# Tokens in chunks of eight rows ahead of layer 1's scans, and layer 0's depthwise conv as diagonal products on TensorE

## The chip, the cores and the metric

The kernel runs on one core of one Trainium2 chip. The time is device microseconds from the first to the last instruction of an execution, the median of several executions. The kernel before took 1817.63 us (1816.01 to 1822.36) when the prediction was made. "Clock" is the share of full speed that was granted to TensorE.

## The reference, cut to what matters

Two layers over 64 x 64 tokens of 96 features. Each layer is a state-space mixer with a residual addition and an MLP with quantized operands with another. Both have the gate, the output norm belongs to layer 0 alone; layer 0's conv is depthwise, layer 1's is a full 192 x 192 one.

```
# layer 0's mixer (the input is normed per token first)
xz = x @ in_proj_w                        # 96 -> 192 and a gate z of 192
xc = conv3x3_depthwise(x_val) + conv_b    # layer 1: dense 3x3, 192 -> 192
u  = silu(xc)
y  = y1 + y2 + back(y3) + back(y4)        # four scans: rows, columns, both ways
y  = layernorm(y, ln_g, ln_b) * silu(z)   # layer 1: no norm here
x  = x + y @ out_proj_w
# the MLP, on a normed x: 96 -> 384 -> 96, fp8 operands
h = relu(q_acc(q_mul(x) @ q_mul(W1).T + q_mul(b1)))
x = x + q_acc(q_mul(h) @ q_mul(W2).T + q_mul(b2))
```

In layer 0 the scan's form, `decay * cumsum(dB_u / (decay + 1e-12))`, makes the output vanish once the decay has run down. The kernel computes the first 160 tokens of each direction, tests whether any later one can matter (`alive`), and for this data skips the rest behind a branch. ln_b is zero and ln_g one in this data.

## The kernel before: the parts concerned

Each phase runs over all 4096 tokens before the next one starts. A norm is five or six instructions over 128 x 3072 elements, and the MLP follows as a loop of eight chunks:

```python
    def norm_tokens(self, pool, eps, dtype):
        # ...
        nc.vector.tensor_reduce(m, res, AX.X, ALU.add)            # 128 x 3072 at once
        # ... centre, square, reduce, root, reciprocal
        nc.vector.tensor_tensor(xn, xc, spread(r), ALU.mult, saturate=False)

    def mlp(self, li, w, out):
        # ...
            xq = self.norm_tokens(wp, self.eps5, FP8)             # all tokens
            # ...
            for b in range(NJ // 4):                              # eight chunks
                # four transposes, a copy, three hidden products with copy, relu, cast,
                # twelve output products, copy, bias, residual
```

Layer 0's conv is VectorE's, nine multiply-adds per channel group:

```python
    def conv_depthwise(self, kp, w, pad, u):
        # ...
                    nc.vector.scalar_tensor_tensor(acc, src, cw[:, tap : tap + 1], acc, ALU.mult, ALU.add)
```

The output product takes 128 tokens as TensorE's weights and moves the 96 columns of the matrix past them:

```python
                for q in range(4):
                    for g in range(2):
                        nc.tensor.matmul(t[:, q, :], by_j[g][:, 4 * b + q, :], self.w_out[g], start=g == 0, stop=g == 1)
```

## Time and profile before

| stage of the kernel before | from | to | us |
|---|---|---|---|
| layer 0 up to the branch (norm, projection, conv, first tokens' scans) | 0 | 218 | 218 |
| layer 0 from the branch to layer 1's conv | 218 | 466 | 248 |
| layer 1's conv and projections | 466 | 668 | 202 |
| transfers alone | 668 | 711 | 43 |
| layer 1's scans | 711 | 1663 | 952 |
| tail (gate, output product, MLP of layer 1) | 1663 | 1815 | 152 |

The bounds are read from a table of windows, of which the prediction shows the lines. Two more lines of that table are the MLP's norm over all tokens, and the eight MLP chunks after it with the store, at the end of the kernel (columns: stretch, length, busy us and count of PE, PEld, DVE, ACT, POOL, clock, DMA share, GB/s).

```profile
1763.00:1784.00 21.00, 0.00 (x0) 0.00 (x0) 14.88 (x13) 4.37 (x3) 2.74 (x1) 0.50 0.07 16
1784.00:1815.00 31.00, 20.23 (x152) 11.54 (x152) 19.97 (x40) 20.05 (x40) 16.73 (x24) 0.67 0.15 52
```

### The profile page before, as it was taken

What the parts mean: (1) busy time and instruction counts of PE and PEld (TensorE: products, weight loads), DVE (VectorE), ACT (ScalarE), POOL (GpSimd) and SP (SyncE); (2) the same over time, 40 slices, a digit from 0 to 9 for tenths busy, and PEclk for the clock granted to TensorE, in tenths of its full rate; (3) what the DMA queues carried; (4) which work ended last, traced back from release to release, by engine and by line L of the source; (5) the groups of instructions that cost most, each with busy time, mean ns of one, the idle gap of its engine ahead of it and who ended that gap; (6) DMA issues with size and microseconds to landing.
All of it is one profiled execution on the core that took longest, in us unless ns stands there. A gap on an engine that the chain in (4) does not pass through costs nothing.

```text
span 1815.0 us, 10479 instructions
## 1 busy us (share of the span) xinstructions
PE 1161.1 (64%) x3146; PEld 468.8 (26%) x3146; DVE 1297.5 (71%) x789; ACT 857.4 (47%) x900; POOL 756.3 (42%) x397
## 2 busy tenths in 40 slices
PE   3102679933999910567677657777667777666784
PEld 2000322622434300222232222222222222222262
DVE  3997367264105053999999999999999999992626
ACT  3023022043104143677766677766677766661205
POOL 0001021031001014676677776677776677752004
PEclk9555565565999955778888888888888888878556
DMA  2014100002002258145434644533553353313301
GB/s 78 0 46 132 36 0 0 0 8 78 5 1 70 75 146 324 46 142 195 139 105 154 205 139 151 185 116 105 178 204 116 139 197 116 104 47 81 116 8 36
DMA packets 52359, 182.39 MB, mean 100 GB/s; under 512 B 24080, under 2 KB 27812, under 8 KB 43940
## 3 DMA queue, kind: packets, MB, share of 16 engines
q1 hardware_dynamic: 44524, 178.44, 29.4%
q10 hardware_dynamic: 7768, 3.19, 0.8%
q8 instruction: 27, 0.44, 0.1%
q14 instruction: 40, 0.33, 0.1%
HBM read 156.39 MB, written 25.19 MB: 100 GB/s over the span
## 4 chain that ended last, share of the span: by engine, by line
DVE 41%; PE 17%; DMA 5%; ACT 4%; issue 4%; SPq 2%; POOL 2%; DVEq 1%; ACTq 1%; POOLq 0%
DVE h0s L798 12%; DVE h1s L798 11%; DVE xws L798 6%; DVE x0s L798 4%; PE cv L337 4%; DVE x1s L798 3%; PE o L1060 2%; DVE x2s L798 2%; PE cv L342 2%; PE cw L349 2%; ACT da L786 2%; SPq L742 2%; DMA dt1s<-dt 1%; PE hs L815 1%; DMA ysa<-y 1%
## 5 line engine op out<-in xcount | busy, mean ns | idle before, releaser
L815 PE MATMUL hs<-hss,ident 128*128 128x512 f32 x384 | 232.4, 690 | 131.9 <-POOL hss L804 89.8
L786 ACT ACTIVATE da<-dt0s,a 128x1024 f32<-128x1024 f32 x168 | 187.6, 1117 | 137.5 <-DVE xws L798 52.3
L786 ACT ACTIVATE da<-dt1s,a 128x1024 f32<-128x1024 f32 x168 | 187.8, 1118 | 114.8 <-DVE xws L798 77.6
L804 POOL TENSOR_TENSOR hss<-h1s,xws 128x1024 f32<-128x1024 f32 x96 | 224.4, 2375 | 23.7 <-DVE xws L798 12.6
L798 DVE TENSOR_TENSOR_SCAN xws<-da,xws 128x1024 f32<-128x1024 f32 x96 | 224.2, 2335 | 8.3
L816 PE MATMUL hs<-h0s,ident 128*128 128x512 f32 x384 | 221.4, 661 | 5.1 <-DVE h0s L798 5.1
L798 DVE TENSOR_TENSOR_SCAN h1s<-da,h1s,xws 128x1024 f32<-128x1024 f32 x72 | 169.2, 2350 | 9.5
L815 PEld LDWEIGHTS hs<-hss,ident 128*128 128x128 f32 x384 | 74.4, 211 | 272.7 <-issue 104.2
L418 POOL TENSOR_TENSOR du<-u,dts 128x1024 f32<-128x1024 f32 x6 | 17.3, 2883 | 231.5 <-DVE dts L530 227.2
L816 PEld LDWEIGHTS hs<-h0s,ident 128*128 128x128 f32 x384 | 81.5, 213 | 114.3 <-issue 102.5
L828 POOL TENSOR_TENSOR hc0s<-hc0s,cs 128x1024 f32<-128x1024 f32 x32 | 75.4, 2357 | 81.3 <-ACT hc0s L823 67.8
L828 POOL TENSOR_TENSOR hc2s<-hc2s,cs 128x1024 f32<-128x1024 f32 x32 | 75.4, 2357 | 78.2 <-ACT hc2s L823 67.9
L828 POOL TENSOR_TENSOR hc1s<-hc1s,cs 128x1024 f32<-128x1024 f32 x32 | 75.4, 2355 | 77.8 <-ACT hc1s L823 64.9
L1113 POOL CAST xb<-lnxn 128x3072 bf16<-128x3072 fp8e5 x2 | 5.5, 2742 | 207.4 <-DVE lnxn L143 119.9
L798 DVE TENSOR_TENSOR_SCAN h1s<-da,xws 128x1024 f32<-128x1024 f32 x24 | 54.7, 2278 | 51.6 <-DMA cs<-bc 48.1
L769 POOL TENSOR_TENSOR x0s<-x0s,dus 128x1024 f32<-128x1024 f32 x32 | 75.0, 2357 | 37.7 <-DMA dus<-du 26.3
L839 PE MATMUL acc<-hc0s,fold 128*32 128x512 f32 x128 | 40.6, 719 | 76.2 <-POOL hc0s L828 76.2
L839 PE MATMUL acc<-hc1s,fold 128*32 128x512 f32 x128 | 40.6, 719 | 75.2 <-POOL hc1s L828 75.2
L839 PE MATMUL acc<-hc2s,fold 128*32 128x512 f32 x128 | 39.7, 704 | 67.5 <-POOL hc2s L828 67.5
L769 POOL TENSOR_TENSOR x2s<-x2s,dus 128x1024 f32<-128x1024 f32 x32 | 75.1, 2358 | 13.5 <-DMA cs<-bc 8.0
L769 POOL TENSOR_TENSOR x1s<-x1s,dus 128x1024 f32<-128x1024 f32 x32 | 75.1, 2362 | 12.5 <-DMA cs<-bc 8.2
L775 ACT COPY xws<-x0s 128x1024 f32<-128x1024 f32 x32 | 61.5, 1952 | 36.2 <-DMA x1s<-bc 36.2
(193 smaller groups left out, 2414.9 us busy)
## 6 DMA issues: line engine op xcount, KB each, us to landing
cs<-bc SPq DMA_DIRECT2D x384, 128.0 KB, 2.6
x0s<-bc SPq DMA_DIRECT2D x32, 512.0 KB, 4.9
x1s<-bc SPq DMA_DIRECT2D x32, 512.0 KB, 4.9
x2s<-bc SPq DMA_DIRECT2D x32, 512.0 KB, 4.9
dus<-du SPq DMA_DIRECT2D x24, 512.0 KB, 7.9
dt1s<-dt SPq DMA_DIRECT2D x40, 256.0 KB, 3.9
dt0s<-dt SPq DMA_DIRECT2D x40, 256.0 KB, 3.1
u<-u SPq DMA_DIRECT2D x3, 2048.0 KB, 6.3
```

The lines of the kernel that those rows point to most:

```text
L337: nc.tensor.matmul(t, cw[0][:, tap, 0:P], image(0, slice(0, P), n, tap), start=tap == 0, stop=False)
L342: nc.tensor.matmul(t, cw[1][r, tap, 0:P], image(1, r, n, tap), start=False, stop=tap == 8)
L349: nc.tensor.matmul(out[m][to], cw[0][:, tap, P:DI], image(0, slice(0, P), c + m + h * half, tap), start=tap == 0, stop=False,)
L769: keep(nc.gpsimd.tensor_tensor(x, x, du[:, part[j]], ALU.mult))
L775: keep(nc.scalar.copy(grid(xw)[:, w, :], cols(xs[i % 3])[:, w, :]))
L786: nc.scalar.activation(das[i, s], dt[o][:, part[j]], AF.Exp, scale=self.a6[:, g, k : k + 1])
L798: keep(nc.vector.tensor_tensor_scan(to, da, x, start, ALU.mult, ALU.add))
L804: nc.gpsimd.tensor_tensor(cols(hs)[:, w, :], grid(first[1])[:, w, :], grid(xw)[:, w, :], ALU.add)
L815: keep(nc.tensor.matmul(t, self.ident, hs[:, s], start=True, stop=False))
L816: keep(nc.tensor.matmul(t, self.ident, first[0][:, s], start=False, stop=False))
L828: keep(nc.gpsimd.tensor_tensor(t, t, c[:, part[j]], ALU.mult))
L839: nc.tensor.matmul(accs[g][GC * q : GC * q + GC, m // NQ, :], self.fold4, hcs[(NS * i + a) % 3][:, h * CH : (h + 1) * CH], start=k == 0, s ...
```

## The change

The intent: tokens flow in chunks of 512 (eight rows), so that the norm, the products and the MLP of different chunks overlap on different engines, and no phase waits for all tokens. Layer 0's conv leaves VectorE: it becomes nine products with diagonal matrices on TensorE, 64 x 64 so that four run at a time, and the image's edges go first, so that the first tokens' scans start early and run beside the rest. The gate and a product of gate and norm bias move ahead of the branch. The scattered column writes of layer 1's step sizes become whole rows. The core of the diff, with cuts and with comments added:

```diff
+    def norm_chunk(self, pool, c, eps, dtype, name):   # 128 x 384, one chunk
     ...
+            ue = self.conv_ends(ep, pm, pad)            # the edges' conv
+            x = self.scan_ends(ep, pe, ue)              # first tokens, on VectorE
+            self.conv0(vp, pm, pad)                     # the whole conv, on TensorE
+            self.gate0(vp, pm, xt, pad)                 # gate, and its product with the bias
+            self.add_ends(pm, x)                        # 80 short products sum the states
     ...
-                    nc.vector.scalar_tensor_tensor(
-                        acc, src, cw[:, tap : tap + 1], acc, ALU.mult, ALU.add
-                    )
+                        nc.tensor.matmul(ab[c][r], self.diag[0][r, tap], self.image(pad, 0, r, c, tap), **ends)
     ...
+            def after(s):
+                c0 = s // 2 * 4 + s % 2
+                for c in (c0, c0 + 2):
+                    self.mlp_chunk(0, c, tp, lp, po, ph, pt)
+                    xn = self.norm_chunk(lp, c, self.eps6, F32, f"c{c}")
     ...
+                    self.in_proj(pa, "a", xt, self.pad1, c, f"1{c}")
+            for s in range(NCH // 2):
+                self.mixed(s, tp, lp, pa, po)           # output norm and product of two chunks
+                if s:
+                    after(s - 1)
+            after(NCH // 2 - 1)
     ...
+            for c in range(NCH):                        # the tail
+                o = po.tile([P, 4, CD], F32, tag="o", name=f"o1{c}")
+                for j in range(4):
+                    at = slice(c * CH + j, (c + 1) * CH, 4)
+                    for g in range(2):
+                        nc.tensor.matmul(o[:, j, :], y[g][:, at], w_out[g], start=g == 0, stop=g == 1)
+                nc.vector.tensor_tensor(self.res[:, c], self.res[:, c], o, ALU.add)
+                self.mlp_chunk(1, c, tp, lp, po, ph, pt)
+                nc.sync.dma_start(ov[:, c], self.res[:, c])
```

## The prediction

> **What bounds the kernel now**
>
> I read the page's slices first, then the chain that ended last in order of time, then a table of windows cut where that chain changes character, and last the timeline inside those windows. The slices show two different programs in one span:
>
> ```profile
> span 1815.0 us, 10479 instructions
> ...
> PE   3102679933999910567677657777667777666784
> ...
> DVE  3997367264105053999999999999999999992626
> ...
> PEclk9555565565999955778888888888888888878556
> ```
>
> Before the sixteenth slice, and in the last three, one engine at a time is busy and TensorE's granted clock is mostly about half. In between VectorE is at 9 in every slice. The windows give the sizes (columns: stretch, its length, busy us and instruction count of PE, PEld, DVE, ACT, POOL, then clock, DMA share, GB/s):
>
> ```profile
> 0.00:51.00 51.00, 21.47 (x64) 12.22 (x64) 19.41 (x18) 17.71 (x22) 1.87 (x18) 0.97 0.23 69
> 51.00:138.00 87.00, 0.42 (x1) 0.00 (x0) 84.65 (x24) 12.69 (x8) 0.00 (x0) 0.51 0.06 24
> 138.00:218.00 80.00, 31.13 (x154) 20.24 (x154) 44.81 (x57) 16.37 (x12) 6.32 (x14) 0.54 0.24 75
> 218.00:291.00 73.00, 58.34 (x64) 15.15 (x64) 44.43 (x37) 15.70 (x24) 17.60 (x14) 0.57 0.09 22
> 291.00:324.00 33.00, 31.57 (x33) 6.34 (x32) 24.16 (x33) 11.47 (x18) 2.93 (x2) 0.50 0.00 0
> 324.00:367.00 43.00, 41.98 (x128) 32.10 (x128) 5.94 (x11) 0.00 (x0) 0.00 (x0) 0.50 0.00 0
> ...
> 466.00:668.00 202.00, 175.17 (x639) 63.56 (x637) 56.27 (x49) 51.02 (x63) 17.30 (x6) 0.91 0.17 57
> 668.00:711.00 43.00, 0.00 (x0) 0.00 (x0) 0.00 (x0) 9.17 (x6) 18.17 (x8) 0.50 0.92 317
> 711.00:1663.00 952.00, 662.59 (x1536) 247.09 (x1536) 892.73 (x384) 644.12 (x626) 652.27 (x281) 0.83 0.40 136
> 1663.00:1678.00 15.00, 0.22 (x1) 0.25 (x2) 0.21 (x2) 0.65 (x1) 0.00 (x0) 0.54 0.76 189
> 1678.00:1719.00 41.00, 31.20 (x32) 6.09 (x32) 29.75 (x47) 10.75 (x17) 0.00 (x0) 0.50 0.44 135
> 1719.00:1763.00 44.00, 42.96 (x128) 32.35 (x128) 5.39 (x11) 0.00 (x0) 0.00 (x0) 0.50 0.00 0
> ```
>
> Read as phases: layer 0's norm and input projection to 51; its depthwise conv, VectorE alone, 87 us; the first tokens' scans, 80; layer 0's output norm, gate and output product to 367, mostly TensorE at half clock; MLP, the next norm and in_proj to 466; layer 1's conv and projections, 202; a DMA-only hole of 43; the scans, 952; the tail, 152. The scans run VectorE 892.73 of 952 us and the diff leaves them as they are, so at most 863 us of the span can move.
>
> Three timeline lines and one of the chain size the parts:
>
> ```profile
> 60.92 61.62 DVE L462 SCALAR_TENSOR_TENSOR u<-pad,cw,u 128x4096 f32<-128x4096 f32 x14
> 527.96 7.96 PE L359 MATMUL cw<-pad,cw 64*64 64x512 f32 x72
> 668.12 5.91 SPq L308 DMA_DIRECT2D dt<-dtc  x2
> 669.23 10.05 DMA dt<-dtc
> ```
>
> An f32 product is two MATMUL records. Layer 1's 128x128 conv products take 0.43 us a record at full clock (36 records in 15.6 us), 0.87 a product; its 64x64 products show 72 records, 36 products, in 7.96 us: four at a time, 0.88 a group. The gate products at half clock take 31.32 us for 16, 1.96 each. The output products take 0.33 a record at half clock (41.98 over 128).
>
> **What the Trainium skill says**
>
> "TensorEngine Tiling (Array Packing)", Tiling Modes: a 64x64 split gives four independent tiles. The trace agrees, 36 products in the time of nine.
>
> "TensorE: Matmul & The Clock Gate", Part 1: the array runs at half clock until a window of about 3.4 us was busy, and falls back after an idle one. The trace agrees in kind (0.50 in the gate stage, 0.91 over layer 1's conv), and adds that the gate stage, 31.57 of 33 us busy, never warmed. Its products sit 1.96 us apart where two cold records need 1.71. So a stage with a small bubble at every product may stay cold, and I do not count on warmth where products wait for another engine.
>
> "DMA: Bandwidth & Descriptors", Specifications: line rate needs pieces of at least 512 B. In 640 to 720 us, 9008 of 11184 packets are below that; the two writes at 668.12 scatter 128-byte pieces, and the traffic from 670 to 680 was 118 GB/s against 365 in the next ten.
>
> "ScalarE: Activation LUTs", Table sets: functions of different sets cost a table load at each switch; 1.28 us each here, not the page's 2.7. The new code batches the gate's sigmoids ahead of layer 0's back part, so sqrt is alone there.
>
> **The change, part by part**
>
> *Front of layer 0 (218 us now).* The norm goes by chunk of 512 tokens, eight of them. A 128x384 VectorE add takes 0.55, so reduce, centre, reduce and scale are about 2.1 with the small ops, plus 0.69 for the pad copy: 2.8 x 8 = 22, and some 6 of new constants and weight casts. The first input chunk lands near 4 us; pads complete at about 38 instead of 54.
>
> The 87 us conv leaves VectorE. First only the edges: 36 steps of three 64x64 products of 192 columns, 192/512 of 0.88 = 0.33 each, weight loads showing at that size, say 0.45: 16 us. Sigmoid and product, 3: the first tokens stand near 57 instead of 138. Their chain is unchanged (54 us from 138 to the last VectorE product), so it ends near 112, with some conv evacuation between.
>
> Beside it TensorE does the whole conv: two halves x four turns x nine taps = 72 groups x 0.88 = 63 us, warm because dense. Then work it did later before, the gate (16 x 0.87 = 14), and a new product of gate and bias, 128 records at 0.2 warm (transposes, 32 in 6.19 us, show that rate) to 0.33 cold, 34 in the middle. The summing of states is 160 short records instead of 128 in 20 us: 17. With 8 for the small projections, TensorE's sum from 38 is 16 + 63 + 8 + 14 + 34 + 17 = 152: 190. VectorE's additions to y and the branch add 7: 197. So the first branch comes only 21 us sooner although 87 us of VectorE work vanish: TensorE becomes this stage's bound. The gate and half the output work are then already paid.
>
> *Back of layer 0 to layer 1's conv (218 to 466, 248 us).* Per chunk TensorE has 3.5 wide products for centring (28 in all), 16 one-column variance products and 8 output products (128 records each sort), the MLP (2.5), four transposes, two in_proj products. Warm: 28 x 0.87 = 24; 128 x 0.19 = 24; 128 x 0.2 = 26; 20; 6; 14: 114. Cold, with 1.96 and 0.33: 55 + 38 + 42 + 25 + 11 + 31 = 202. VectorE: about 9.7 a chunk, 78; ScalarE about 54. The reciprocals over 128x512, 3.35 each, 27 in all, become 128x4. I take a mixed clock, 155, plus filling and draining the two-chunk pipeline, 15 to 20: 172. It ends near 369 instead of 466, 97 earlier.
>
> *Layer 1.* Same products, 202 us. In the hole, the group-1 column write becomes whole rows and the two scattered writes go: 10 of 43. The first scan starts at 369 + 202 + 33 = 604.
>
> *Scans.* 952, ending at 1556.
>
> *Tail (152).* Store and first loads, now in quarters, 12; gate products cold 8 x 3.9 = 31; output and MLP by chunk, 5.4 + 2.5 cold, 8 x 7.9 = 63, warm 44; 8 more for the last chunk and its store. The norm's 21 us alone and the MLP's 31 disappear under TensorE. About 108.
>
> Sum: 1556 + 108 = 1664; less a few for overlap I cannot place, 1660, which is 158 us or 8.7% below 1817.63.
>
> **Rivals**
>
> *A: TensorE stays cold in the back part.* For: every stage from 51 to 449 but the MLP shows 0.50 to 0.57, and one-column products are nearly all weight loads. Against: transposes, MLP and in_proj come in bursts. Then 202 + 20, and a colder bias product and tail: +65, about 1725.
>
> *B: the chunks overlap well and latency is hidden.* For: VectorE's 78 and ScalarE's 54 are far below TensorE; layer 1's in_proj at 450 stayed warm with small bubbles. Then the back part costs 130, the front 185 and the tail 98: about 1600.
>
> *C: the long chain per chunk (centre, square, variance, root, product, norm, MLP, norm, in_proj) serialises, in-order engines waiting on each other.* I count 35 us of latency a chunk from the durations above; with pairs only one stage apart, four pairs x 55 = 220 and no gain beyond A: 1720.
>
> *D: the conv's evacuation starves behind VectorE's first-token chain*, six PSUM buffers fill and TensorE stops. VectorE was busy 41.95 of the 55 us of that chain (138 to 193), so 12 evacuations of 0.7 fit its gaps: at worst +15.
>
> **Range and chances**
>
> The scans fix 952 us and layer 1's conv 202; the uncertain 500 have A and C on one side (+60) and B on the other (-60): 1595 to 1730 for 8 in 10. Within 2% would need 1781, every removed phase given back; slower has no mechanism I see except the two together with table thrash. Faster 0.95, same 0.04, slower 0.01.
>
> **What would show it**
>
> The conv as 64x64 products at about 0.22 us a record four at a time, its first branch near 197 with TensorE above 85% busy from 40 on; the first scan near 604; scans within 952 +- 10; TensorE's clock from 197 to 369 between 0.6 and 0.8; the hole about 33 us without packets of 128 B. Wrong if the branch comes after 215, if TensorE is under 60% busy in the back part (C), if its clock there is 0.5 (A), or if the scans themselves move.

## The result, and the profile after

The changed kernel took 1884.06 us (1880.96 to 1884.46, four runs), the kernel before 1817.76 in the same rounds: slower, ratio 1.0357 with a 95% interval of 1.0335 to 1.0379. The prediction said 8.7% faster, with 0.95 on faster; it was wrong in sign, and the time lies far outside its range.

The page of the changed kernel, its slices:

```profile
span 1882.7 us, 12714 instructions
...
PE   6889989667599960277577766777667775776754
...
DVE  5452112333302341899999999999999999981633
...
PEclk8987555555599975588888888888878888786555
```

The windows cut at the same events as those of the kernel before (same columns):

```profile
65.00:153.00 88.00, 77.02 (x452) 26.62 (x452) 48.77 (x61) 26.96 (x32) 0.00 (x0) 0.88 0.25 72
153.00:222.00 69.00, 68.98 (x165) 38.13 (x163) 13.63 (x22) 9.54 (x16) 0.00 (x0) 0.57 0.04 12
222.00:250.00 28.00, 28.00 (x134) 25.34 (x134) 0.51 (x1) 0.00 (x0) 0.00 (x0) 0.50 0.00 1
...
262.00:513.00 251.00, 183.90 (x527) 107.50 (x527) 78.70 (x179) 55.70 (x110) 18.76 (x32) 0.55 0.06 14
513.00:718.00 205.00, 176.63 (x641) 64.16 (x639) 56.42 (x49) 56.04 (x65) 17.37 (x6) 0.90 0.17 57
718.00:760.00 42.00, 0.00 (x0) 0.00 (x0) 1.60 (x1) 10.92 (x7) 18.52 (x8) 0.50 0.92 340
760.00:1709.00 949.00, 661.91 (x1536) 246.93 (x1536) 890.52 (x384) 642.54 (x623) 651.90 (x280) 0.84 0.41 136
...
1724.00:1883.00 159.00, 102.21 (x312) 53.85 (x312) 69.64 (x120) 42.45 (x76) 40.27 (x48) 0.50 0.20 48
```

In the slices TensorE is now busy from the first slice on, VectorE is mostly idle until the scans, and the clock is at half from the fifth slice to the eleventh, in the two of the transfers and in the last three. The windows, set against the prediction's own sum (the first row joins the windows up to layer 0's first centring product at 260):

| stage | before | predicted | measured | measured less predicted |
|---|---|---|---|---|
| layer 0 up to the branch | 218 | 197 | 260 | +63 |
| from the branch to layer 1's conv | 248 | 172 | 253 | +81 |
| layer 1's conv and projections | 202 | 202 | 205 | +3 |
| transfers alone | 43 | 33 | 42 | +9 |
| scans | 952 | 952 | 949 | -3 |
| tail | 152 | 108 | 174 | +66 |
| sum | 1815 | 1664 | 1883 | +219 |

Three stages carry 210 of the 219 us. None of them gained, although 87 us of VectorE's conv, both long norms and the slow reciprocals are gone. TensorE is busy 1354 us in all instead of 1161.

The tail shows one of the causes plainly. One chunk of it, from a timeline (start, length, engine, line, and what the engine waited for before):

```profile
1808.26 0.66 PE L170 MATMUL tf<-identb,xb 128*96 128x128 bf16 x4 [5.51 <-POOL xb L1333]
...
1809.59 1.01 PE L1339 MATMUL h<-xf,w 96*128 96x512 bf16 x2 [0.67 <-ACT xf L171]
...
1812.07 2.18 PE L1275 MATMUL o<-two,ys 128*128 128x96 f32 x6
...
1818.64 0.55 DVE L1276 TENSOR_TENSOR res<-res,o 128x384 f32<-128x384 f32 x1 [5.76 <-PE o L1275]
...
1819.58 0.55 DVE L153 TENSOR_REDUCE lnmb<-res 128x4 f32<-128x384 f32 x1
...
1822.84 0.56 DVE L162 TENSOR_TENSOR lnxnb<-lnxcb,lnrb 128x384 fp8e5<-128x384 f32 x1
1823.56 0.51 POOL L1333 CAST xb<-lnxnb 128x384 bf16<-128x384 fp8e5 x1 [9.99 <-DVE lnxnb L162]
1824.12 0.45 PEld L170 LDWEIGHTS <-xb 128*96 128x96 bf16 x4 [5.75 <-POOL xb L1333]
```

The next chunk's output product (L1275) sits in the middle of this chunk's MLP on TensorE; its addition, the norm that needs it, the cast and the transposes follow one after another, each engine waiting for the one before. From transposes to transposes it is 15.86 us, against at most 3.9 us a chunk before. Layer 0's back part has the same form: its last input projections (L281) start 17.4 us apart, with nothing between them on TensorE but one chunk's transposes and MLP.

```profile
457.86 3.78 PE L281 MATMUL in<-xt,w_in 96*128 96x512 f32 x4 [0.67 <-ACT xt L171]
475.26 3.78 PE L281 MATMUL in<-xt,w_in 96*128 96x512 f32 x4 [0.67 <-ACT xt L171]
```

In the front the conv stage shows two stalls of TensorE, in the timeline of that engine:

```profile
94.58 0.59 PE L535 MATMUL leastt<-ident,least 128*1 128x128 f32 x2 [5.26 <-DVE least L533]
117.45 2.62 PE L393 MATMUL cab<-pad,diag 64*64 64x512 f32 x4 [5.39 <-DVE ua L375]
```

The first is a one-column product for the branch's test, which waits for the first tokens' chain on VectorE. The second is the conv's next output buffer: its earlier content waits to be taken out by VectorE (L375), which is at work on that same chain until 116.7.

The groups of the window 153 to 222 give the cost of the gate and bias product (columns: busy us, mean ns of one):

```profile
L443 PE MATMUL ob<-wb,pad 128*128 128x96 f32 x64 | 23.8, 481 | 0.0
L444 PE MATMUL ob<-wb,pad 64*128 64x96 f32 x64 | 21.7, 487 | 0.0
```

128 records in 45.5 us are 0.36 each. The load of their weights alone takes 0.32, as the first of these lines says (ns: shortest/median/longest; then the time of the first and the last, us):

```profile
L443 PEld LDWEIGHTS ob<-wb,pad x64: 307/329/332, 157.3 to 220.6; 128*128 128x128 f32 x64
L568 PEld LDWEIGHTS ya<-bce,ident x64: 285/333/337, 211.2 to 253.2; 128*128 128x128 f32 x64
L915 PEld LDWEIGHTS cv<-pad,cw x144: 186/189/337, 512.4 to 640.7; 128*128 128x128 f32 x144
```

The other two are f32 loads of as many columns which lie side by side in memory, at half clock (the summing of states) and almost all at full clock (layer 1's conv): 0.33 and 0.19. The gate and bias product loads every fourth column, and its loads hardly depend on the clock. The first of these products ran at full clock, the rest at half, and TensorE did not stand in between:

```profile
157.30:162.50 5.20, 5.18 (x17) 3.87 (x16) 2.00 (x3) 1.20 (x2) 0.00 (x0) 1.00 0.01 5
162.60:210.30 47.70, 47.70 (x106) 24.56 (x106) 8.16 (x13) 4.18 (x7) 0.00 (x0) 0.50 0.00 0
```

From 159.56 to 162.10, at full clock, a product of two records comes every 0.64 us; from 164.24 to 168.51, at half, every 0.71. So they run at the pace of the weight loads, and the clock counts for a tenth.

### The profile page after: what moved, and what is told of

Read it like the earlier page. It is cut to its first block, busy times and chain, and to the rows that moved or that the text cites. A ratio compares the mean times of both kernels' runs of the same rounds, so it can differ in the third digit from the quotient of the medians.

```text
span 1882.7 us, 12714 instructions
## 1 busy us (share of the span) xinstructions
PE 1354.4 (72%) x4074; PEld 593.7 (32%) x4074; DVE 1192.3 (63%) x909; ACT 871.1 (46%) x978; POOL 753.8 (40%) x412
## 4 chain that ended last, share of the span: by engine, by line
DVE 40%; PE 25%; ACT 6%; DMA 6%; POOL 3%; issue 3%; SPq 2%; DVEq 0%; POOLq 0%; ACTq 0%
DVE h0s L1114 11%; DVE h1s L1114 11%; DVE xws L1114 4%; DVE x0s L1114 3%; PE cv L915 3%; DVE x2s L1114 3%; DVE x1s L1114 2%; PE o L1275 2%; ACT da L1102 2%; DMA cs<-bc 2%; PE cv L920 2%; PE cw L928 2%; PE in L281 2%; SPq L1058 2%; DMA dt1s<-dt 1%
## 5 line engine op out<-in xcount | busy, mean ns | idle before, releaser
L990 POOL TENSOR_TENSOR du<-u,dt 128x1024 f32<-128x1024 f32 x6 | 17.4, 2895 | 195.6 <-ACT z L669 106.9
L1344 POOL CAST h<-h 128x512 fp8e5<-128x512 f16 x48 | 29.4, 614 | 134.9 <-DVE h L1342 134.9
L1333 POOL CAST xb<-lnxnb 128x384 bf16<-128x384 fp8e5 x16 | 8.6, 535 | 179.7 <-DVE lnxnb L162 179.7
```

## The experiments

The theories. **S**: the chunk order serialises, so that each chunk's chain of norm, transposes, MLP and addition runs alone. **T**: TensorE is the bound, because work moved to it and its products are slower than I took them. Under T there are two readings: the loading of tokens as weights sets the pace, or the low clock does. **D**: the conv starves behind VectorE's first-token chain. Sixteen kernels ran, each timed in three rounds. The kernel before had a median of 1817.8 to 1818.7 in all of them. Differences of less than 5 us between runs are not read. All outputs are right.

| run | median us | ratio to before, 95% interval |
|---|---|---|
| the changed kernel | 1884.06 | 1.0357 (1.0335 to 1.0379) |
| tail_staged | 1838.89 | 1.0115 (1.0094 to 1.0136) |
| back_staged | 1820.42 | 1.0009 (0.9988 to 1.0031) |
| no_bias | 1822.23 | 1.0023 (1.0003 to 1.0043) |
| conv_evac | 1880.32 | 1.0335 (1.0315 to 1.0356) |
| tail_bufs | 1889.32 | 1.0391 (1.0369 to 1.0412) |
| orders | 1777.01 | 0.9780 (0.9756 to 0.9804) |
| conv_split | 1869.16 | 1.0265 (1.0236 to 1.0294) |
| all3 | 1763.42 | 0.9684 (0.9661 to 0.9707) |
| least_late | 1880.36 | 1.0340 (1.0323 to 1.0358) |
| ob_wide | 1859.90 | 1.0228 (1.0211 to 1.0245) |
| conv_split2 | 1856.67 | 1.0215 (1.0197 to 1.0232) |
| wide_all | 1722.70 | 0.9451 (0.9398 to 0.9504) |
| best1 | 1706.30 | 0.9386 (0.9355 to 0.9416) |
| prewarm | 1719.56 | 0.9452 (0.9421 to 0.9483) |
| prewarm2 | 1726.37 | 0.9465 (0.9418 to 0.9513) |
| best2 | 1713.13 | 0.9416 (0.9387 to 0.9445) |

### The order of the chunks

**tail_staged.** The same instructions in the tail, in another order. `mlp_chunk` is cut into its norm and its body:

```diff
             for c in range(NCH):
                 # ... output product and addition
-                self.mlp_chunk(1, c, tp, lp, po, ph, pt)
-                nc.sync.dma_start(ov[:, c], self.res[:, c])
+            xb = [self.mlp_norm(1, c, lp, NCH) for c in range(NCH)]
+            for c in range(NCH):
+                self.mlp_body(1, c, tp, po, ph, pt, xb[c])
+                nc.sync.dma_start(ov[:, c], self.res[:, c])
```

> The changed kernel with only the order of the last stage altered: all eight output products with their additions first, then the norms of all chunks, then the MLPs of all chunks; same instructions, shapes and buffers. Before the run the last stage (from the end of the scans) is 174 us and each chunk's norm and MLP take 15.8 us one after another, with TensorE busy 9 of them. Theory S (the chunk order serialises: one chain of norm, transposes, MLP, addition per chunk, in-order engines): the MLPs overlap as in the kernel before (3 us a chunk), the stage falls to about 125, the total by 40 to 60 us (1825 to 1845). Theory T (TensorE itself is the bound, its 102 us of products at half clock): nothing to gain but the idle, less than 10 us (1874 to 1884).

45 us came off, as S said. One thing beyond the order changed: the tile `xb` got eight buffers for two, since eight norms wait at once (here and in back_staged); tail_bufs below answers for buffers in the tail. The transposes of successive chunks, in TensorE's timeline:

```profile
1799.25 0.63 PE L170 MATMUL tf<-identb,xb 128*96 128x128 bf16 x4
...
1802.67 0.63 PE L170 MATMUL tf<-identb,xb 128*96 128x128 bf16 x4
...
1804.18 0.66 PE L170 MATMUL tf<-identb,xb 128*96 128x128 bf16 x4 [0.19 <-POOL xb L1339]
```

After a first one at 1785.69, seven such groups lie between 1799.25 and 1817.09, 3.0 us apart on the mean where they were 15.9. The stage is about 130 us.

**back_staged.** The same in layer 0's back part:

```diff
-            for s in range(NCH // 2):
-                self.mixed(s, tp, lp, pa, po)
-                if s:
-                    after(s - 1)
-            after(NCH // 2 - 1)
+            for s in range(NCH // 2):
+                self.mixed(s, tp, lp, pa, po)
+            xb = {c: self.mlp_norm(0, c, lp, NCH) for c in order}
+            for c in order:
+                self.mlp_body(0, c, tp, po, ph, pt, xb[c])
+            for c in order:
+                # second norm, transposes, in_proj
```

> The changed kernel with only the order of layer 0's back part altered: output norm and product of all chunks first, then all MLP norms, all MLPs, then all second norms and input projections; same instructions, shapes and buffers. The stage is 251 us now, TensorE busy 184 of it at clock 0.55. Theory S: the 67 us of TensorE's idle time mostly go, the stage is 200 to 215 and the total 1835 to 1850. Theory T: products at half clock are the bound and the stage keeps 240 or more, total above 1873.

64 us came off; the stage is 191, better than S expected. Its windows:

```profile
258.00:384.00 126.00, 126.00 (x303) 77.30 (x304) 27.59 (x76) 16.61 (x35) 3.53 (x9) 0.55 0.08 17
384.00:449.00 65.00, 51.52 (x228) 28.00 (x227) 46.92 (x105) 36.55 (x75) 20.62 (x27) 0.67 0.09 25
```

The MLP, the second norm and the input projection of all chunks take 65 us together. The 126 us before them are TensorE's without a gap: there theory T holds.

**tail_bufs.** The order as in the changed kernel, but more buffers in the tail:

```diff
+            pa_ctx.close()                              # the gate's PSUM goes back first
-            po, ph, pt: bufs 2, 2, 1
+            po, ph, pt: bufs 3, 3, 2
-            al1 bufs=2, at1 bufs=3
+            al1 bufs=4, at1 bufs=6
```

> The changed kernel with the order of the last stage as it is, but with more buffers there: the gate's PSUM buffers are given back first, then 3 for output products, 3 for hidden products and 2 for transposes (2, 2 and 1 before), four for the norms, six for the MLP's tiles. Theory S-order (the engines' program order makes the chunks wait for one another): within 10 us of the changed kernel's 1884. Theory S-buffers (the tiles are too few, and the order is only what the buffers force): the same gain as the staged order, about 1840.

1889.32, 5 us more than the changed kernel, and its transposes still start 15.5 us apart: in the tail it is the order and not the number of buffers. The Trainium skill has the reason, on the page "PSUM — Partial Sum Buffer", section "Engine vs sequencer instructions": VectorE, ScalarE and GpSimd take their instructions strictly first in, first out, and TensorE's products start and complete in program order. A norm that stands behind this chunk's last steps in VectorE's list waits for them, however many buffers there are. The timeline above agrees: VectorE stood for 5.76 us before L1276, which waited for TensorE's L1275, and did nothing else meanwhile.

**orders.** Both staged orders together.

> Both staged orders together (layer 0's back part and the last stage), everything else as in the changed kernel. Alone they took 45 and 64 us off. If the two are separate serial stages, their gains add: 1884 - 109 = 1775, 2.3% below the kernel before. If they share a cause that the first already removes (the clock of TensorE, transfers), less: above 1790.

1777.01: the gains of 45 and 64 add up (107 measured), and the kernel is 2.2% faster than the one before (the interval, 2.0 to 2.4%, leaves open whether it is more than 2).

### What TensorE does in the front

**no_bias.** The 64 products of gate and bias left out. The result is right only because ln_b is zero here.

```diff
-            for c in (c0, c0 + 2):
-                t = pm.tile([P, 4, CD], F32, tag="m", name=f"ob{c}")
-                self.out_proj(t, self.sz, self.wb, c)
-                nc.vector.tensor_tensor(self.res[:, c], self.res[:, c], t, ALU.add)
```

> The changed kernel without the 64 products of gate and norm bias (the bias is zero in this data, so the result stays right; the kernel would be wrong for other data). Theory T (TensorE bounds the front of layer 0 from 44 to 260 us): 45 us of TensorE work vanish and the branch comes 40 to 50 us earlier, total about 1838. Theory S says nothing of the front; if instead the first tokens' chain on VectorE (ends at 117) or another wait bounds the front, less than 15 us.

62 us came off, more than the 45.5 us of the products themselves. The window from the end of the conv to the branch:

```profile
152.00:200.00 48.00, 42.96 (x196) 27.69 (x192) 13.21 (x30) 9.54 (x16) 0.00 (x0) 0.78 0.06 19
```

48 us where it was 107, at clock 0.78 where it was 0.50 to 0.57. So TensorE bounds the front (T), and these products also slowed their neighbours: with them, the gate's products ran mostly cold; without them, TensorE was busy without a gap from 152.6 to 169 and kept full clock (1.00) to the gate's end.

**ob_wide.** The same result by another shape: the matrix as weights, 512 tokens moving, then a copy and four transposes a chunk.

```diff
-            self.out_proj(t, self.sz, self.wb, c)
+            nc.tensor.matmul(a[0:CD], w[0], y[0][:, chunk(c)], start=True, stop=False)
+            nc.tensor.matmul(a[0:CD], w[1][r], y[1][r, chunk(s)], start=False, stop=True)
+            nc.scalar.copy(sb[0:CD], a[0:CD])
+            for j in range(4):
+                nc.tensor.transpose(t[:, j, :], sb[0:CD, j:CH:4], self.ident[0:CD, 0:CD])
```

> The changed kernel with the 64 narrow products of gate and bias (128 records of 96 columns, each with its own load of 128 tokens as weights, 45 us) done as 16 wide ones (the matrix as weights, 512 tokens moving), a copy and 32 transposes. Weight-load theory (0.64 us a product even at full clock, because the loading of tokens as weights costs more than the product): 16 x 0.87 + 32 x 0.2 = 20 us warm, total 20 to 30 lower. Clock theory (what counts is that TensorE is cold there, and it stays cold): 16 x 1.95 + 32 x 0.27 = 40 us, total within 8 of 1884.

24 us came off, as the weight-load theory said. The clock theory had the clock stay low, and it did not, so this run alone does not part the two; the 0.64 and 0.71 us above do. The groups in the same part:

```profile
L454 PE MATMUL oa<-pad,wb 64*96 64x512 f32 x16 | 10.6, 747 | 1.2 <-DVE pad L419 1.2
L453 PE MATMUL oa<-pad,wb 128*96 128x512 f32 x16 | 10.6, 747 | 0.0
...
L457 PE MATMUL ob<-ident,osb 96*128 96x96 f32 x32 | 6.2, 324 | 5.4 <-ACT osb L455 5.4
```

21.2 and 6.2 make 27.4 us for 45.5. The window from 153 to 200 has the clock at 0.85. The Trainium skill, "TensorE: Matmul & The Clock Gate", section "LDWEIGHTS (loading the stationary operand)", gives the time of a load by its columns alone, P / 1.2 ns, which is 107 ns for 128. An fp8 load of 128 columns takes 0.097 us at full clock (the kernel before, 399 to 408), near the page's figure, and 0.10 to 0.22 at half clock (the changed kernel); an f32 load of as many takes 0.19 to 0.34, by clock and by the distance of its columns, as shown above. A rival is left here: the product may be slow not because tokens are its weights but because every fourth column is loaded. ob_wide changes both, and no run changes the distance alone.

**wide_all.** Both orders, and all three sets of output products (bias, layer 0, layer 1) wide.

> Both staged orders (1777 us), and all three sets of narrow output products (gate and bias, layer 0's output, layer 1's output; 45 us each) done wide with transposes. Weight-load theory: 20 to 25 us less for each, 1705 to 1725. Clock theory: 5 less for each, about 1762.

1722.70, 54 us below the two orders alone, between the two expectations for each set (18 us a set) and near the weight-load one. Its runs lie between 1710 and 1733, with granted clocks of 0.801 and 0.791: a spread of over 1% between runs of one kernel that no edit made, so its differences of a few us are not read. Layer 0's back part is now 170 us (239 to 409). That this is near the 172 of the prediction is luck: it took a staged order and wide products, which the prediction did not have.

### The conv's stalls

**conv_evac.** The conv's results taken out by ScalarE and GpSimd:

```diff
-            nc.vector.scalar_tensor_tensor(u, t, self.vec[g][:, 0:1], sg, ALU.add, ALU.mult)
+            nc.scalar.activation(u, t, AF.Identity, bias=self.vec[g][:, 0:1])
+            nc.gpsimd.tensor_tensor(u, u, sg, ALU.mult)
```

> The changed kernel with the results of layer 0's conv taken out of PSUM by ScalarE (sigmoid, and a copy with bias) and multiplied on GpSimd, so that VectorE's chain of the first tokens has no part in it. Theory D (the conv starves behind that chain): the two TensorE stalls of 5.3 and 5.4 us at 89 and 112 go, TensorE stays at full clock through the conv, the conv takes 65 to 75 us and not 88, total 10 to 25 us less (1859 to 1874). If the stalls only hid slack, or ScalarE's table loads and extra copies take their place: within 5 us.

**least_late.** The one-column product moved behind the conv in TensorE's order:

```diff
             self.conv0(vp, pm, pad)
+            self.check_alive(ep, pe)        # was inside scan_ends, ahead of conv0
             self.gate0(vp, pm, xt, pad)
```

> The changed kernel with one small product moved in TensorE's order: the test whether later tokens matter (a product of one column that waits for the first tokens' chain on VectorE) comes after layer 0's conv and not in the middle of it. In-order theory: the stall of 5.3 us at 89 goes, and with it some of the cold groups after it; the conv's 88 us become 75 to 83 and the total falls by 5 to 12. If the second stall (evacuation behind the same chain, at 112) only grows by what the first loses: within 3 us.

4 us each, about what the no-gain readings named. The stalls did not go. First the line of least_late, then those of conv_evac:

```profile
117.21 2.62 PE L394 MATMUL cab<-pad,diag 64*64 64x512 f32 x4 [15.52 <-DVE ua L376]
```

```profile
94.51 0.38 PE L536 MATMUL leastt<-ident,least 128*1 128x128 f32 x2 [5.00 <-DVE least L534]
120.82 0.72 ACT L377 ACTIVATE y<-uc,d 128x512 f32<-128x512 f32 x1 [4.27 <-POOL uc L376]
123.33 1.97 PE L394 MATMUL cab<-pad,diag 64*64 64x512 f32 x2 [3.07 <-ACT ua L375]
```

With the early wait gone, TensorE fills its six buffers sooner and then waits 15.5 us for the same event at 117. In conv_evac the early wait stays, since it is not for a buffer, and the second is now for ScalarE. ScalarE's own part of the first-token chain was over at 101.1; the take-out stands in its list behind two scalings (L377) that wait 3.56 and 4.27 us for GpSimd's product. That product took 2.1 to 5.0 us while VectorE was at the end of its chain and 1.26 after it. So the wait that theory D names is there in the lines, but each edit put another in its place: what the conv would gain without it is not shown.

**conv_split.** Channels 0 to 127 of the conv on VectorE again (36 multiply-adds of a quarter image), the other 64 on TensorE:

```diff
-                    for c, r in zip(pair, LANES):
-                        nc.tensor.matmul(ab[c][r], self.diag[0][r, tap], self.image(pad, 0, r, c, tap), **ends)
+                    nc.vector.scalar_tensor_tensor(acc, src, self.cw[0][:, tap : tap + 1], acc, ALU.mult, ALU.add)
```

> The changed kernel with half of its conv undone: channels 0 to 127 of layer 0's depthwise conv are nine multiply-adds on VectorE again (36 instructions of a quarter image), the other 64 channels stay diagonal products on TensorE, and so do the first tokens' edges. TensorE loses 288 of 432 records: the conv's group 1 alone should take 32 us for 88. Theory T (the front is bound by TensorE): the branch comes 30 to 55 us earlier than 260, total 1830 to 1855. If VectorE becomes the bound (54 us chain + 40 + 12 evacuations, from 44 on: about 165) the gain stops near 30. Theory that the diagonal products are the good part of the change: slower than 1884.

15 us came off, less than expected. TensorE's conv ended at 107, and then it stood:

```profile
100.00:150.00 50.00, 18.14 (x61) 6.90 (x58) 39.82 (x47) 23.39 (x28) 0.00 (x0) 0.68 0.26 81
```

The gate's evacuation was emitted behind the last step of VectorE's conv. **conv_split2** only swaps these two:

```diff
+            self.gate0(vp, pm, xt, pad)
             # the last step of VectorE's conv: sigmoid, product, scale
-            self.gate0(vp, pm, xt, pad)
```

> As the split conv before (group 0 on VectorE), with the gate and its product emitted ahead of the last step of VectorE's conv. In the first split kernel TensorE idled from 107 to 142, since the gate's evacuation stood behind that step. If that order was what took the gain away, TensorE goes on at about 110: 69 us of gate and bias product, 32 of summing, the branch near 217, total about 1840. If VectorE as such is now the bound: no better than 1869.

27 us came off in all, with the branch at 232 and not 217. One long wait of TensorE is left:

```profile
128.49 1.35 PE L450 MATMUL ob<-wb,pad 128*128 128x96 f32 x4 [20.44 <-DVE pad L426]
```

L426 takes the gate out, on VectorE, and stands behind the first tokens' chain, which ends at 127.7: the wait of theory D once more. Part of the loss was the order of the two steps, the rest is that VectorE's list is full there. **all3** was conv_split with both staged orders:

> Both staged orders and the split conv together. If the three gains are in separate serial stages they add: 1775 less the 30 to 55 of the split conv, 1720 to 1745, 4 to 5% below the kernel before.

1763.42, 14 us below the orders alone: the gains add, and the split conv gave the 15 it gave alone.

### All together, and the clock

**best1.** Both orders, wide products, and conv_split2.

> Both staged orders, the three sets of wide output products and the split conv with the early gate. If the causes are separate, the split conv's 27 us come off 1722.7: about 1695. The bias product is smaller now, so the front has less TensorE work behind VectorE's part; if VectorE's first-token chain and conv then bound the front, no more than 10 us come off: 1710 to 1725.

1706.30, 6.1% below the kernel before and the fastest. The split conv gave 16 us here and not 27: with the smaller bias product there is less TensorE work to bring forward, and TensorE still waits for half of this window:

```profile
105.00:150.00 45.00, 22.50 (x35) 6.14 (x34) 25.43 (x21) 12.62 (x15) 0.00 (x0) 0.55 0.05 13
```

This version keeps the bias product, so it holds for any ln_b.

**prewarm, prewarm2, best2.** The tail's gate products take 1.96 us each at clock 0.50. Is that because TensorE stood still for 14 us before them? Products into an unused tile fill that wait, 14 in prewarm, 38 in prewarm2 (both on wide_all) and in best2 (on best1):

```diff
+            warm = pa.tile([P, 4, CD], F32, tag="a", name="warm")
+            for _ in range(38):
+                nc.tensor.matmul(warm, self.ident, self.res[:, 0], start=True, stop=True)
```

> Both staged orders and wide products (1722.7 us) with 14 products into an unused PSUM tile while TensorE would wait for the last stage's loads (14 us). Theory idle-cold (the granted clock is low because TensorE stood still before): the gate products after them run at full clock, 16 to 20 us for 31, and the total falls by 10 or more. Theory own-bubbles (gate products with a gap at each never warm, as in the kernel before): the dummy products may warm, the gate stays at 1.96 us a product, total within 5 us.

> Both staged orders, wide products, and 38 products of 0.34 us into an unused tile, which fill the wait for the last stage's loads up to the gate's first product. Theory idle-cold: the gate's first products run at full clock (1.0 us and not 1.96 each) and the 31 us of the gate become 18 to 22, total 1708 to 1714 against 1719 to 1723. Theory own-bubbles: the clock falls back within the gate's first few products, the gate takes 28 to 33 us, total within 5 us of 1720.

> The same 38 products in the kernel that has the split conv too (1706.3 us). Idle-cold: 1692 to 1698. Own-bubbles: within 5 us of 1706.

In prewarm they ran too early and TensorE stood another 7.2 us; its clock was at half again, and the run shows nothing of the question. In prewarm2 they reached the gate. TensorE's timeline there:

```profile
1607.58 22.20 PE L1269 MATMUL warm<-res,ident 128*128 128x384 f32 x68
1629.62 3.08 PE L1279 MATMUL z<-xta,tw_in 96*128 96x512 f32 x6
1633.38 4.19 PE L1279 MATMUL z<-xta,tw_in 96*64 96x512 f32 x8 [0.68 <-DVE sga L1284]
...
1641.28 2.13 PE L1279 MATMUL z<-xta,tw_in 96*128 96x512 f32 x4 [2.40 <-DVE sga L1284]
...
1647.47 2.08 PE L1279 MATMUL z<-xta,tw_in 96*128 96x512 f32 x2 [0.16 <-DVE sga L1284]
```

A record x2 is one product. The first products take 1.03 us, warm (the clock was full from 1582 on and stayed so through the filling); then they wait for VectorE, which takes the gate out (L1284), and at 1647 they take 2.08 again. So both theories hold a part: the cold start is from standing still, and the clock is lost again while each product waits for VectorE. The gate took 29 us from its start and not 36. I had counted 0.34 us for a product where that is one of its two records, so the filling ended about 7 us later than the gate began in wide_all (1629.6 against 1622.0), which eats the gain; neither run is faster than the kernel it is built on. At 0.65 us each some 22 would fill the wait and be the clean test, which was not run; as VectorE sets the pace here, not much would be won.

## Why the prediction was wrong

**Right.** The scans did not move (949) and layer 1's conv took 205 for 202; the change leaves their products as they were. The first tokens' chain ended at 116.7 for "near 112". That "TensorE becomes this stage's bound" in the front was right, and so was the kind of each rival: the products stayed cold (A), the chains serialised (C), the conv starved (D). They were named as alternatives, one at a time; all three came.

**Order, 147 us of miss in two stages, 109 of it shown.** The step that failed is "plus filling and draining the two-chunk pipeline, 15 to 20: 172" in the back part, and its twin, "The norm's 21 us alone and the MLP's 31 disappear under TensorE", in the tail. I took the overlap that the change intends as done. The sources emit one chunk after another, and each engine runs in order, so there is one chain at a time: 17.4 us a chunk in the back, 15.9 in the tail. The same instructions staged took 64 and 45 us less, and in the tail more buffers did nothing. Rival C had the mechanism, with a size of 220 for the stage (measured: 253), and I weighed it only against the back part. The tail has the same code and I gave it no chain at all. The sign that I had set for C, TensorE under 60% busy in the back part, did not come: it was busy 183.90 of 251 us, 73%, and the chains were there all the same. The kernel before showed the price of a chunk in overlap, at most 3.9 us; what a chunk costs alone had to be added up along one chain.

**The rate of the narrow products.** The step "128 records at 0.2 warm (transposes, 32 in 6.19 us, show that rate) to 0.33 cold, 34 in the middle" is mis-sized: 45.5 us, 0.36 a record. A transpose's rate is not that of an f32 product whose weights are every fourth of 512 tokens: that load alone takes 0.31 to 0.33, warm or cold. So the kernel before's "0.33 a record at half clock" was no cold rate that could halve. The same wrong 0.2 stands in the back part and, as "warm 44", in the tail. Done wide, the three sets gave 54 us. (A slip without effect: the variance products are 8 a chunk, not 16; the sum has their 128 records right.)

**The rest of the front.** Of the +63, pads complete at 44.5 for 38 is 6; the edges 19 for 16 is 3; conv with the small projections 88 for 71 is 17, of which the two stalls are 10.7; gate and bias product 69 for 48 is 21; the summing of states 32 for 17 is 15, all of it at half clock (28 of 28 us busy in its window, clock 0.50; in no_bias half of its records ran at full clock, 80 in 10 us). Rival D was capped "at worst +15" from VectorE's idle time in the chain; the longest single stall of the conv that the runs showed was 15.5. The mistake was to count it as a rival and not in the sum.

**The clock.** "I take a mixed clock, 155" was kinder than what came: 0.55 in the back, and still 0.55 in its staged form where TensorE never stands (126 of 126 us). That stage is mostly narrow and one-column products. In the front such products lost the clock without any wait: it fell at 162.6, five us after the first of them, with TensorE busy throughout, and in no_bias, without them, the gate kept it. Taking them away brought the clock there from 0.57 to 0.78 (no_bias) and 0.85 (ob_wide). Whether it is their weight loads or their short streams of columns that the clock does not count is not shown.

**The transfers.** "10 of 43" came out as about 3. In the timelines of the two kernels:

```profile
668.12 5.91 SPq L308 DMA_DIRECT2D dt<-dtc  x2
679.35 1.14 SPq L742 DMA_DIRECT2D x0s<-bc  x2
```

```profile
717.26 1.11 SPq L890 DMA_DIRECT2D dt<-dtc  x1
725.02 1.12 SPq L1058 DMA_DIRECT2D x0s<-bc  x2
```

From the last write to the first load it is 7.8 us for 11.2. The write in rows is cheaper to issue, but the load waits for its landing all the same, and from there to the first scan it is 33 us in both.

**What stays open.** best1 is 46 us above my 1660. Its branch came at 221 for 197, and its tail took 124 for 108, at half clock throughout. How far TensorE could be kept warm was not settled, and neither was what the distance of the loaded columns costs.

## What to carry to other kernels

Cutting a phase into chunks does not make the chunks overlap: on engines that run in order the overlap is in the order of emission, so add up one chunk's chain from end to end and ask which instruction of the next chunk stands between. Before moving work to an engine, take the rate from a product of the same shape and the same operand as weights, and sum that engine's whole stage with what it will wait for. And when a rival is a wait of known size, put it into the sum; here three rivals came true together.

## What the Trainium skill lacked or had wrong

- "TensorE: Matmul & The Clock Gate", "LDWEIGHTS (loading the stationary operand)": P / 1.2 ns, 107 ns for 128 columns, without a word on the clock or the distance of the columns; the page's next section has loads scale with the column count and not with bytes. At full clock fp8 took 0.097 us for 128 columns, f32 twice that, 0.19 (0.33 at half clock); f32 of every fourth column took 0.31 to 0.33 at either clock and sets the pace of products with few moving columns (0.36 us a record of 96 columns).
- The same page, Part 1: busy for about 3.4 us is said to release the clock. In layer 0's staged back part TensorE was busy 126 of 126 us in the records at a mean clock of 0.55, in the summing of states 28 of 28 at 0.50, and in the gate stage the clock fell from full to half with TensorE busy 5.18 of 5.20 us before and 47.70 of 47.70 after. So "busy" in the records is not what releases it or holds it. Dense f32 products held a full clock for 22 us, and it fell after 17 us of products with waits of 0.2 to 2.4 us between them.
- "PSUM — Partial Sum Buffer", "Engine vs sequencer instructions" states the strict order but not what follows from it for loops over chunks: 15.9 us a chunk in one order and 3.0 in another, with the same instructions; more buffers in the first order left it at 15.5.
